# Expert layers of a four-layer gated model: results added to the tokens' rows in DRAM by indirect transfers, instead of gathered back

## The chip, the cores and the metric

The kernel runs on one core of one Trainium2 chip. The metric is device time in microseconds (us), the median of several runs. A profile of one execution goes with it; its time is a little longer than its span, which runs from the first to the last instruction recorded. Engines are named as in the profile: PE (matmuls), PEld (their weight loads), DVE (vector), ACT (scalar), POOL (GpSimd), SP (the sync engine, which here only issues transfers).

## The reference

Two sequences of 1024 tokens, 256 values each, pass through four layers. Each layer adds a gated cross-attention to 64 context rows and then a gated feed-forward part. `x` is the residual stream.

```python
x = x + jnp.tanh(g_xattn[0]) * _L0_xattn_ref(_layernorm(x), ctx_1024, ...)
x = x + jnp.tanh(g_ffn[0]) * _L0_ffn_ref(_layernorm(x), ...)     # 8 experts, each token goes to its best one
x = x + jnp.tanh(g_xattn[1]) * _L1_xattn_ref(_layernorm(x), ctx_1024, ...)
x = x + jnp.tanh(g_ffn[1]) * _L1_ffn_ref(_layernorm(x), ...)     # 8 experts, every token through all
x = x + jnp.tanh(g_xattn[2]) * _L2_xattn_ref(...)
x = x + jnp.tanh(g_ffn[2]) * _L2_ffn_ref(...)    # best expert, at most 384 tokens each
x = x + jnp.tanh(g_xattn[3]) * _L3_xattn_ref(...)
x = x + jnp.tanh(g_ffn[3]) * _L3_ffn_ref(...)    # best two experts, at most 320 tokens each
```

An expert is two matrix products with a bias and a function between them. For layer 2, with `h` the normalized tokens:

```python
logits = h @ router_w.T
probs = softmax(logits); chosen_e = argmax(probs); chosen_p = max(probs)
pos = (running count of chosen_e before this token)          # its place in the expert's buffer
kept = pos < C
out = gelu(buf[e] @ w1[e] + b1[e]) @ w2[e] + b2[e]           # buf[e]: the tokens kept for expert e
y = out[chosen_e, pos] * (chosen_p * kept)
```

Layers 0 and 3 are alike, without a limit in layer 0, and with two choices per token and normalized weights in layer 3. All of it is float32.

## The kernel before

The residual stream stays in the chip's SBUF for the whole run, as `xs`: 16 tiles of 128 tokens, in four groups of four (`NT` = 16, `NG` = 4). The layers follow each other in program order. A framework orders each engine's instructions and sets the waits; its planned times decide how instructions of neighbouring parts interleave. A transfer is issued from the queue of an engine: SP for plain ones, ACT for a few constants, POOL for indirect ones, which take one row per index. Each queue is worked off in order, so an instruction that waits holds what is behind it.

Layers 0, 2 and 3 send tokens to experts, in the same steps:

- `normed` (L185) normalizes all groups (`norm_group`, `stats`): `h` by token, `hT` transposed. `keep_tokens` (L703) writes `h` to a DRAM buffer `hd`, from SP.
- `route` (L608) computes for each token its expert, its weight and its rank among the expert's tokens. From these comes a slot number: the row of the token in the experts' buffers.
- `invert` (L671) turns "slot of each token" into "token of each slot" by matmuls with one-hot matrices (`ohl`, `ohh`; L685 to L695). The result, `idx` (L700), holds for every slot of 128-row tiles the number of its token; an unused slot gets 0.
- `gather_T` (L711) gathers the tokens of a tile from `hd` by an indirect transfer on POOL (L716), transposes them on PE (L725) and copies them to `xT` on DVE and ACT (`evac`, L138).
- `ffn` (L729) does the two products (`ps_m`, through `mm256`, L193; then `ps_y`, L741), adds the bias on DVE (`y_ff`, L746) and writes the tile from SP to a DRAM buffer `yb` (L747).
- `combine` (L750), after all experts: for each tile of tokens and each choice it gathers the results' rows from `yb` (L756, POOL) and adds them, times the weight, to `xs` (L760, DVE). `yg` has four buffers.

In layer 0 (`moe0`, L784) the tokens of an expert fill whole tiles, 23 in all (`L0_NTILE`). Which expert's weights a tile needs is known only on the chip, so the weights are gathered too, by POOL (`rows_of`, L841): two of 1 MB (`w`), and two small ones (`b1j`, `b2j`). In layers 2 and 3 (`moe_capacity`, L864) each expert has three tiles (128, 128, 128 rows; 128, 128, 64 in layer 3), and weights are loaded from SP (`load_w`). `wpool` has six weight buffers, `xgp` six token buffers, `yp` four result buffers.

After layer 0's experts stand the set-up of the next attentions (`heads1.setup`, `xattn2_setup`), `combine`, and the middle (L1135): layer 1 with its dense experts, and the attention of layer 2, worked off by groups; `group` (L541, L600) writes the last update of `xs` there. Weights of the middle are loaded from SP (L991, L994). After layer 2's experts follow the attention of layer 3 (`heads_xattn`) and its experts, whose last lines send `xs` to the output from SP (L1206).

Of the kernel before, what the change touches and what calls it, by code (L numbers as in the profile page):

```python
# [17 lines left out]
P = 128  # L18
B, S, D = 2, 1024, 256
SK = 64  # L20
N = B * S
# [20 lines left out]
def kernel(ctx: ExitStack, tc: tile.TileContext, a: dict, out: bass.AP):  # L42
# [34 lines left out]
    partid = int_ramp([P, 1], [[0, 1]], 0, 1, "partid")  # L77
    rev8 = int_ramp([P, E], [[-1, E]], E, 0, "rev8")
# [592 lines left out]
    def invert(one, pm, slots, ntile):  # L671

        ps = pm.tile([P, 512], F32, name="ps_m")
        for i, slot in enumerate(slots):
# [13 lines left out]
            ohh = one.tile([P, NT, ntile], F32, name="ohh")  # L688
            V.tensor_tensor(
                ohh, ramp[:, :ntile].unsqueeze(1).to_broadcast([P, NT, ntile]),  # L690
                bc(hi, ntile), ALU.is_equal,
            )
            V.tensor_mul(ohh, ohh, bc(tokid, ntile))
            for t in range(NT):
                T.matmul(  # L695
                    ps[:, :ntile], lhsT=ohl[:, t, :], rhs=ohh[:, t, :],
                    start=(i == 0 and t == 0), stop=(i == len(slots) - 1 and t == NT - 1),
                )
        idx = one.tile([P, ntile], I32, name="idx")
        V.tensor_copy(idx, ps[:, :ntile])  # L700
        return idx

    def keep_tokens(hs, name):  # L703
        hd = dram.tile([N, D], F32, name=name)
        for g in range(NG):
            nc.sync.dma_start(
                hd[g * GW : (g + 1) * GW, :].rearrange("(t p) d -> p t d", p=P), hs[g]
            )
        return hd

# [18 lines left out]
    def ffn(pools, xT, w1, w2, b1, b2, widths, func, yb, row0):  # L729
# [8 lines left out]
        for w in widths:  # L738
# [8 lines left out]
            nc.sync.dma_start(yb[row0 + at : row0 + at + w, :], y[:w, :])  # L747
            at += w

    def combine(yp, yb, choices):  # L750

        for t in range(NT):
            xt = xs[:, t, :]
            for slot_i, wgt in choices:
                yg = yp.tile([P, D], F32, name="yg")
                G.indirect_dma_start(  # L756
                    out=yg, out_offset=None, in_=yb[:, :],
                    in_offset=bass.IndirectOffsetOnAxis(ap=slot_i[:, t : t + 1], axis=0),
                )
                V.scalar_tensor_tensor(xt, yg, wgt[:, t : t + 1], xt, ALU.mult, ALU.add)  # L760
# [23 lines left out]
    def moe0():  # L784
        with ExitStack() as es:
# [3 lines left out]
            hd = keep_tokens(hs, "hd0")  # L789
# [29 lines left out]
            slot_i = one.tile([P, NT], I32, name="slot0_i")  # L819
            V.tensor_copy(slot_i, slot)  # L820
# [18 lines left out]
            idx = invert(one, pm, [slot], L0_NTILE)  # L839
# [8 lines left out]
            yb = dram.tile([L0_NTILE * L0_W, D], F32, name="yb0")  # L848
# [462 lines left out]
```

## Time and profile before

| | us |
|---|---|
| median of three runs | 2472.63 (2470.77 to 2479.15) |
| the profiled execution | 2466.53 |
| its span | 2464.7 |
| PE busy | 2173.3 (88%) |
| DVE busy | 1259.3 (51%) |
| POOL busy | 1019.3 (41%) |
| ACT busy | 755.6 (31%) |
| L741 PE, products `ps_y` | 252.8 |
| L756 POOL, gathers of results | 61.6 in 64 instructions |
| L760 DVE, adding them to `xs` | 38.9 in 64 instructions |
| L716 POOL, gathers of tokens `xg<-hd_L` | 45.1 in 48 instructions |

Rows of groups give the line, engine and operation, what is written and read, how many there are, the busy time, the mean of one in ns, and the engine's idle time ahead of them with what ended most of it. A POOL row of an indirect transfer is the time of its issue, not of the transfer. The chain that ended last is followed back from the last instruction; in order of time, each line has a start, a length and the engine or transfer that was waited for. In a table of windows every stretch of time has its length, then each engine's busy time and number of instructions, the granted PE clock, the busy share of the 16 DMA engines, and GB/s.

### The profile page before, as it was taken

How to read it: one execution, taken by the hardware profiler on the slowest of the kernel's cores; microseconds unless marked ns; L12 is line 12 of the kernel's file. 1: busy time of each engine (PE TensorE's matmuls, PEld its weight loads, DVE VectorE, ACT ScalarE, POOL GpSimd, SP SyncE). 2: the span in 40 equal slices, each digit the busy share in tenths (PEclk: the TensorE clock that was granted, in tenths of full speed). 3: DMA queues.
4: the chain of work that ended last, by engine and by line, in shares of the span. 5: the costliest groups of instructions: out<-in, count | busy, mean ns of one | idle time of the engine just before them, and what ended most of it. 6: DMA issues, size and time to landing. Idle time of an engine off the chain costs nothing.

```text
span 2464.7 us, 27973 instructions
## 1 busy us (share of the span) xinstructions
PE 2173.3 (88%) x10132; PEld 1776.8 (72%) x10132; DVE 1259.3 (51%) x2725; ACT 755.6 (31%) x1431; POOL 1019.3 (41%) x1220
## 2 busy tenths in 40 slices
PE   5569995999999999999999999999779968878991
PEld 3268883688888788887788878888567745566771
DVE  7940005676566866566756565656620028651002
ACT  1003430443333533335333343333212213221220
POOL 3315555146666356663466655666111020001104
PEclk9759996899999999999999999999869989867995
DMA  2028982012322122321222222222413440012313
GB/s 84 0 71 301 312 309 88 9 60 87 92 87 77 44 77 88 91 87 49 73 90 90 86 78 82 89 86 86 137 54 124 120 143 5 9 44 75 124 52 108
DMA packets 91177, 232.20 MB, mean 94 GB/s; under 512 B 13792, under 2 KB 32736, under 8 KB 80672
## 3 DMA queue, kind: packets, MB, share of 16 engines
q1 hardware_dynamic: 71216, 157.70, 20.2%
q0 software_dynamic: 14816, 68.53, 8.5%
q10 hardware_dynamic: 5008, 4.18, 0.5%
q8 instruction: 81, 1.33, 0.2%
q14 instruction: 56, 0.46, 0.1%
HBM read 213.20 MB, written 17.17 MB: 93 GB/s over the span
## 4 chain that ended last, share of the span: by engine, by line
PE 77%; DVE 9%; DMA 3%; issue 3%; POOL 3%; ACT 2%; DVEq 0%; POOLq 0%; ACTq 0%; SPq 0%
PE ps_b L1022 13%; PE ps_m L193 11%; PE ps_y L741 10%; PE ps_a L1022 9%; PE ps_e L1022 9%; PE ps_b L1067 6%; PE ps_a L1067 4%; PE ps_e L1067 4%; PE ps_y L429 2%; PE ps_y L193 2%; DMA yg<-yb_L,at_i 1%; PE ps_tr L181 1%; PE ps_y L381 1%; PE ps_m L695 1%; DVE st L149 1%
## 5 line engine op out<-in xcount | busy, mean ns | idle before, releaser
L1022 PE MATMUL ps_b<-xsum,w 128*128 128x256 f32 x1536 | 386.9, 380 | 2.3 <-DVE c L1048 2.2
L1022 PEld LDWEIGHTS ps_b<-xsum,w 128*128 128x128 f32 x1536 | 289.4, 190 | 47.1 <-issue 4.6
L929 POOL TENSOR_TENSOR w<-w 128x256 f32<-128x256 f32 x192 | 141.1, 735 | 382.2 <-DMA w<-in_L_Wu_dram 193.9
L1022 PE MATMUL ps_a<-hT,w 128*128 128x256 f32 x1024 | 268.6, 382 | 0.6 <-DVE hT L142 0.6
L193 PE MATMUL ps_m<-xT,w 128*128 128x128 f32 (+2 forms) x1248 | 247.9, 358 | 13.8 <-DVE xT L142 13.7
L741 PE MATMUL ps_y<-w,mid 128*128 128x256 f32 (+1 forms) x1136 | 252.8, 379 | 0.0
L193 PEld LDWEIGHTS ps_m<-xT,w 128*128 128x128 f32 x1248 | 183.4, 195 | 73.1 <-DVE xT L142 21.3
L741 PEld LDWEIGHTS ps_y<-w,mid 128*128 128x128 f32 (+1 forms) x1136 | 206.6, 184 | 38.9 <-issue 2.7
L974 ACT COPY u<-ps_b 128x512 f32<-128x512 f32 (+1 forms) x192 | 98.7, 514 | 406.9 <-PE ps_b L1067 260.7
L1022 PEld LDWEIGHTS ps_a<-hT,w 128*128 128x128 f32 x1024 | 193.3, 191 | 29.7 <-issue 3.2
L746 DVE TENSOR_TENSOR y_ff<-ps_y,b 128x256 f32<-128x256 f32 (+1 forms) x48 | 20.3, 423 | 312.7 <-PE ps_y L741 312.7
L716 POOL DMA_INDIRECT xg<-hd_L,idx x48 | 45.1, 939 | 319.8 <-PE ps_tr L725 180.7
L930 POOL TENSOR_TENSOR w<-w 128x256 f32<-128x256 f32 x192 | 167.7, 873 | 0.1
L931 POOL TENSOR_TENSOR w<-w 128x256 f32<-128x256 f32 x192 | 165.3, 861 | 0.0
L932 POOL TENSOR_TENSOR w<-w 128x256 f32<-128x256 f32 x192 | 158.9, 828 | 14.4
L1022 PE MATMUL ps_e<-xsum,w 128*128 128x256 f32 x512 | 133.6, 382 | 0.0
L1022 PE MATMUL ps_e<-hT,w 128*128 128x256 f32 x512 | 133.2, 380 | 0.0
L1067 PE MATMUL ps_b<-t,w 128*128 128x256 f32 x512 | 131.8, 381 | 0.9 <-DVE accT L1085 0.9
L1067 PE MATMUL ps_a<-b,w 128*128 128x256 f32 x512 | 132.0, 379 | 0.0
L956 ACT COPY ps_b<-ps_a 128x512 f32<-128x512 f32 (+1 forms) x192 | 96.1, 501 | 108.5 <-DVE b L1052 64.1
L1084 POOL TENSOR_TENSOR m<-m,accT 128x256 f32<-128x256 f32 x60 | 72.1, 1201 | 126.5 <-ACT m L962 112.8
L1049 DVE TENSOR_TENSOR b<-b,c 128x512 f32<-128x512 f32 x128 | 116.1, 907 | 3.8
(300 smaller groups left out, 3785.0 us busy)
## 6 DMA issues: line engine op xcount, KB each, us to landing
w<-in_L_Wg_dram SPq DMA_DIRECT2D x64, 512.0 KB
w<-in_L_Wu_dram SPq DMA_DIRECT2D x64, 512.0 KB
w<-in_L_Wd_dram SPq DMA_DIRECT2D x64, 512.0 KB
w<-in_L_W_dram SPq DMA_DIRECT2D x32, 1024.0 KB
yb_L<-y_ff SPq DMA_DIRECT2D x40, 128.0 KB
hd_L<-h SPq DMA_DIRECT2D x8, 512.0 KB
yb<-y_ff SPq DMA_DIRECT2D x23, 128.0 KB
xs<-in_x_dram SPq DMA_DIRECT2D x4, 512.0 KB
```

The source lines that it names most:

```text
L193: T.matmul(ps, lhsT=lhs(c), rhs=rhs(c), start=(c == 0), stop=(c == n - 1))
L741: T.matmul(ps[:w, :], lhsT=mid[:, f, at : at + w], rhs=w2[:, f, :], start=(f == 0), stop=(f == NF - 1),)
L929: G.tensor_add(s[0], a21, a22)
L930: G.tensor_sub(s[1], s[0], a11)
L931: G.tensor_sub(s[2], a11, a21)
L932: G.tensor_sub(s[3], a12, s[1])
L956: A.copy(self.b, self.pa)
L974: A.copy(u2, self.b)
L1022: T.matmul(ps[:, q * 256 : (q + 1) * 256], lhsT=lhs[kind][:, q, :], rhs=xr[kind], start=(first and q == 0), stop=True, skip_group_check=True,)
L1049: V.tensor_mul(m[name], m[name], c)
L1067: T.matmul(ps, lhsT=wd[kind][:, q, :], rhs=m["rhs"][kind][:, q * 256 : (q + 1) * 256], start=(clear and q == 0), stop=True, skip_group_che ...
L1084: G.tensor_add(sb, sb, acc[:, i, j])
```

## The change

Each expert layer first writes the residual stream to a second DRAM buffer `xd` (`keep_rows`, which takes the place of `keep_tokens`). `invert` also returns the weight of each slot (`wsl`), by twice as many columns in its matmuls. `ffn` multiplies a result tile by these weights on DVE and adds its rows to their tokens' rows of `xd`, with one indirect, adding transfer on POOL. Unused slots have weight zero; `idx` sends slot row p of them to a spare row N + p, so that the rows of one transfer are distinct, and both buffers have 128 such rows, zeroed. `combine` and `yb` are gone. At the end of layers 0 and 2 `xs` is reloaded from `xd`; at the end of layer 3 `xd` is copied to the output, from SP and ACT.

```diff
+    spare = int_ramp([P, 1], [[0, 1]], N, 1, "spare")
+    tokoff = int_ramp([P, NT], [[P, NT]], -N, 1, "tokoff")
+    zeros = const.tile([P, D], F32, name="zeros")
+    V.memset(zeros, 0.0)
...
-    def invert(one, pm, slots, ntile):
+    def invert(one, pm, slots, wgts, ntile):
...
-            ohh = one.tile([P, NT, ntile], F32, name="ohh")
+            ohh = one.tile([P, NT, 2, ntile], F32, name="ohh")
...
-            V.tensor_mul(ohh, ohh, bc(tokid, ntile))
+            V.tensor_sub(lo, tokoff, lo)
+            V.tensor_mul(ohh[:, :, 0], ohh[:, :, 1], bc(lo, ntile))
+            V.tensor_mul(ohh[:, :, 1], ohh[:, :, 1], bc(wgt, ntile))
             for t in range(NT):
                 T.matmul(
-                    ps[:, :ntile], lhsT=ohl[:, t, :], rhs=ohh[:, t, :],
+                    ps[:, : 2 * ntile], lhsT=ohl[:, t, :],
+                    rhs=ohh[:, t].rearrange("p a j -> p (a j)"),
...
-        V.tensor_copy(idx, ps[:, :ntile])
-        return idx
-
-    def keep_tokens(hs, name):
-        hd = dram.tile([N, D], F32, name=name)
+        V.tensor_scalar(idx, ps[:, :ntile], spare, None, ALU.add)
+        wsl = one.tile([P, ntile], F32, name="wsl")
+        V.tensor_copy(wsl, ps[:, ntile : 2 * ntile])
+        return idx, wsl
+
+    def keep_rows(name, parts):
+
+        hd = dram.tile([N + P, D], F32, name=name)
         for g in range(NG):
             nc.sync.dma_start(
-                hd[g * GW : (g + 1) * GW, :].rearrange("(t p) d -> p t d", p=P), hs[g]
-            )
+                hd[g * GW : (g + 1) * GW, :].rearrange("(t p) d -> p t d", p=P), parts(g)
+            )
+        nc.sync.dma_start(hd[N:, :], zeros)
         return hd
+
+    def residual(g):
+        return xs[:, g * TG : (g + 1) * TG, :]
+
+    def reload(xd):
+        for g in range(NG):
+            nc.sync.dma_start(
+                residual(g), xd[g * GW : (g + 1) * GW, :].rearrange("(t p) d -> p t d", p=P)
+            )
...
             V.tensor_add(y[:w, :], ps[:w, :], b2[:w, :])
-            nc.sync.dma_start(yb[row0 + at : row0 + at + w, :], y[:w, :])
+            V.tensor_scalar_mul(y[:w, :], y[:w, :], wsl[:w, j0 + s : j0 + s + 1])
+            G.indirect_dma_start(
+                out=xd[:, :],
+                out_offset=bass.IndirectOffsetOnAxis(ap=idx[:w, j0 + s : j0 + s + 1], axis=0),
+                in_=y[:w, :], in_offset=None, compute_op=ALU.add,
+            )
             at += w
-
-    def combine(yp, yb, choices):
...
-            hd = keep_tokens(hs, "hd0")
+            hd = keep_rows("hd0", lambda g: hs[g])
+            xd = keep_rows("xd0", residual)
...
-            combine(yp, yb, [(slot_i, wgt)])
+            reload(xd)
...
             if then:
                 then(pm, "ps_m")
-            combine(yp, yb, choices)
+                reload(xd)
+        return xd
...
-    moe_capacity("L3", 2, e_bias[:, 1, :], 2, L3_CAP, 7, AF.Relu)
-
-    ov = out.rearrange("b (t p) d -> p (b t) d", p=P)
+    xd = moe_capacity("L3", 2, e_bias[:, 1, :], 2, L3_CAP, 7, AF.Relu)
+
+    of = out.rearrange("b s d -> (b s) d")
     for g in range(NG):
-        nc.sync.dma_start(ov[:, g * TG : (g + 1) * TG, :], xs[:, g * TG : (g + 1) * TG, :])
+        eng = nc.sync if g % 2 else nc.scalar
+        eng.dma_start(of[g * GW : (g + 1) * GW, :], xd[g * GW : (g + 1) * GW, :])
```

## The prediction

> **What bounds the kernel now.** I read the page's shares first (PE busy 88% of the span), then the chain of waits in order of time, to find the places where PE is not what ends last. Three lie around this change: the ends of the three expert layers, where results are gathered back. The table of windows gives each expert loop and what follows it up to PE's next real work (for layer 3, up to the end).
>
> ```profile
> core 0: us, PE busy (x) PEld busy (x) DVE busy (x) ACT busy (x) POOL busy (x), PEclk, DMA share, GB/s
> 184.40:374.90 190.50, 175.74 (x1153) 159.27 (x1154) 14.09 (x46) 73.42 (x207) 104.89 (x111) 0.98 0.86 298
> 375.30:420.00 44.70, 14.35 (x68) 10.18 (x67) 30.60 (x65) 0.06 (x1) 33.62 (x40) 0.60 0.37 121
> 1828.40:2009.00 180.60, 175.73 (x694) 128.16 (x695) 15.01 (x33) 42.13 (x73) 20.74 (x22) 0.98 0.39 121
> 2009.00:2039.30 30.30, 4.39 (x21) 2.88 (x20) 19.61 (x72) 0.34 (x1) 15.25 (x16) 0.61 0.44 143
> 2242.10:2413.00 170.90, 165.34 (x686) 119.67 (x686) 14.06 (x32) 37.13 (x72) 19.61 (x21) 0.98 0.28 91
> 2413.00:2464.70 51.70, 0.00 (x0) 0.00 (x0) 15.50 (x32) 0.00 (x0) 30.49 (x32) 0.52 0.46 123
> ```
>
> The loops (rows 1, 3, 5) are PE's, with little else near its limit in layers 2 and 3. Layer 0's loop is different: DMA share 0.86. The exits (rows 2, 4, 6) last 44.7, 30.3 and 51.7 us with PE nearly or wholly idle. The chain inside the last exit says what fills it:
>
> ```profile
> 2413.00 1.90 DMA yb_L<-y_ff
> ...
> 2415.76 2.21 DMA yg<-yb_L,at_i
> ...
> 2423.27 2.99 DMA yg<-yb_L,at_i
> ...
> 2429.52 4.95 DMA yg<-yb_L,at_i
> ...
> 2456.09 2.90 DMA yg<-yb_L,at_i
> ```
>
> One landing of the last result, then 32 gathers at POOL's pace: a gather lands 2.2 to 3.0 us after its start, 5 us when others are in flight. Last, POOL's queue in layer 0's loop, which the change lengthens:
>
> ```profile
> 230.56 0.95 POOL L842 DMA_INDIRECT b2j<-in_L_b_dram,ex_i  x1 [2.07 <-DVE xT L142]
> 231.81 0.95 POOL L716 DMA_INDIRECT xg<-hd,idx  x1 [0.30 <-issue]
> 233.06 0.94 POOL L842 DMA_INDIRECT w<-in_L_W_dram,wrow  x1 [0.30 <-issue]
> 234.31 0.94 POOL L842 DMA_INDIRECT w<-in_L_W_dram,wrow  x1 [0.30 <-PE ps_m L193]
> 235.55 0.95 POOL L842 DMA_INDIRECT b1j<-in_L_b_dram,wrow  x1 [0.30 <-issue]
> 238.57 0.94 POOL L842 DMA_INDIRECT b2j<-in_L_b_dram,ex_i  x1 [2.06 <-DVE xT L142]
> ```
>
> Five issues of 0.95 + 0.30 = 1.25 us make 6.25 us of an 8.01 us tile; POOL idles 2 us, then waits for the tile's end.
>
> **What the Trainium skill says.** "DMA: Bandwidth & Descriptors", section "SDMA does more than copy": an add during a transfer is done by a compute unit in the data stream; no rate is given, and no run here shows one yet. Section "Rules for kernel authors": nothing holds the destination between an accumulate's read and write, so the earlier DMA's semaphore must be waited for. The built order has that: each scatter on POOL waits for the one before to land. Section "Queues, rings and completion order": an engine takes a ring's descriptors in order. The trace agrees: the last gather of layer 0 stood behind weight loads on POOL's queue and landed after 5.30 us.
>
> **The change, part by part.** The profiled execution took 2466.53 us for a span of 2464.7; the median of the runs is 2472.63, so 6.1 above. I sum against the former.
>
> (1) Layer 3's exit. Removed: 51.7 us. Added: the weight multiply, 0.4 (128x256, as h L173 at 0.35, plus its wait); the last scatter; the copy to the output. Scatter: unknown. Below, a gather's 2.2 us; above, I carry 12. I take 3.5, a gather's 2.2 to 3.0 plus a destination read. The three last scatters start 3.5 us apart (PE's 3.46 us per tile), so they just don't queue. The output now goes DRAM to DRAM, 4 x 512 KB on two queues. Not in the trace; the page's section "Latency and other measured facts" gives about 210 GB/s per direction for copies between HBM tensors: 2.1 MB is 10 us (estimate), plus 2.0 fixed (its section on the SWDGE path). Below: 6 us, engines at 8 KB in 0.31 us; above: 20. Sum 0.4 + 3.5 + 12 + 0.1 = 16. Gain 51.7 - 16 = 35.7.
>
> (2) Layer 0's exit. After: multiply, behind one setup instruction on DVE, 0.8; scatter 3.5; reload of the first 512 KB, 4.0 (the last out DMA, issued at 2460.74, ended the span at 2464.7); norm of four tiles on DVE, 4 x (0.40 + 0.16) + about 2 of small ones + 4 x 0.35 = 6; setup instructions mixed into it (kT, vT, wos), 2.5; transposes and hT 2.3. Sum 19.1 against 44.7: gain 25.6. Setup's matmuls lie inside this; the first DVE statistic stands before the last setup instructions, so they too wait for the reload, which is why I add their 2.5. The reload stands before the next weights on SP: they issue some 5 us later, are needed some 40 us on, and hide behind attention.
>
> (3) Layer 2's exit. Multiply and setup 0.8, scatter 4.5 (a 1 MB weight load runs beside it), reload 4, norm 6 with 2 of the next group's mixed in, transposes and hT 1.8: 19 against 30.3. About 1 to 2 us of norm work that was done between gathers now comes later, on a busy DVE. Gain 10.
>
> (4) Layer 0's loop. POOL gets a sixth issue: 7.5 of 8.0 us, still under. But the built order puts xg of tile j+2 behind scatter j, and scatter j behind y_ff j and the landing of scatter j-1. Behind it queue b1, b2, xg and the next weights. From tile j's last matmul: scatter at +1.05, b1 2.3, b2 3.55, xg 4.8; the transposes that read it start at +7.84 at today's pace. So a gather has 3.0 us, where it had 5.9 before; in the last seven tiles w2 and a multiply ahead of xT come between too, and it has 1.8. And 2 MB of weights ahead in the ring take 7 us at 298 GB/s. I get 0.2 to 0.5 us late per tile, which the longer tile then partly forgives, 0.8 in the last seven: loss 8 us (bounds 0, and 35 at 1.5 us per tile). Unlike before, yb's 128 KB writes on SP are gone, which pays for part of the scatter's traffic.
>
> (5) Before each loop, invert. Per slot one more multiply of ohh (0.55) and a small subtract (0.17), less a cast: 0.6 on the way to idx, four slots: +2.5. The matmuls grow from 24 to 48 columns; they are 0.22 us apart, as are those with 256 columns, so the width is free; if not, 4 x 1 us.
>
> (6) Costed at nothing: the copy of xs to xd. In layer 0 its four issues precede hd on SP at about 130 us, 50 us before the first gather. In the middle they would block weight loads on SP if xs were late: counted through the built order, they stand after loads issued at 874.5, 1197.3 and 1474.1, xs is ready at 875.7, 1206.2 and 1481.1, and the next loads issue at 881.0, 1207.6 and 1483.9. Free, by a margin of 1 to 5 us; without it, a stall of a few us at PE. Zero rows: six writes while SP only waits. The multiply in layers 2 and 3 stands after xT in DVE's order, DVE busy 8%. Scatters in layers 2 and 3: one each 7.0 to 7.3 us, against 3.5; gathers are two experts ahead.
>
> Sum: 35.7 + 25.6 + 10 - 8 - 2.5 = 61. 2466.5 - 61 = 2405.7 against the profile, 2411.8 against the median. I say 2408.
>
> **The rivals.** (A) Layer 0's loop turns from PE-bound to bound by POOL's order and ring: a tile of 9.5 us, gain (2) lost. For: 0.86 DMA share and 0.5 us of POOL left; an accumulating issue may cost POOL more than 0.95. Against: weights are two tiles ahead, and a longer tile loosens the ring. Cost 35 instead of 8: 2435.
> (B) Tails longer: scatter 6 us, output 20. The last three scatters then queue (+7.5), the other exits lose 2.5 each, the output 8: 2428.
> (C) Slower: the serialized scatters set the pace. 24, 24 and 23 of them follow each other by landing; a landing of x us costs 24(x - 7.3) + 24(x - 7.0) + 23(x - 8.0) once above these. It eats the 61 us at about 8.1 us; at 10, 2600. For it: reading and writing rows in DRAM for each of 128 rows, whose rate nothing shows. Against: a 128 KB write with 1 KB packets passes the engines in 0.5 us here, so it would have to be over ten times that.
> (D) No change: all exits are refilled by later waits; PE then starts no earlier. Layer 3's exit speaks against it: nothing follows it.
>
> **How the numbers follow.** Forecast 0.62 (its own range 2388 to 2425); A 0.17, B 0.10, C 0.08, D 0.02, 0.01 for mixtures below the range. 2385 to 2445 leaves out C, D and half of the worse A: just under 2 in 10. Faster 0.90, same 0.02, slower 0.08, with 0.3% (7.4 us) as what a measurement can tell.
>
> **What would show it.** Last y_ff to span's end about 16 us, not 51.7; PE's next start after layers 0 and 2 about 19 us on, not 44.7 and 30.3; layer 0's tile period 8.0 to 8.5 us, its lost time before ps_tr, waiting for xg; scatter landing about 3.5 us. Wrong if a scatter lands after over 7 us, if POOL's scatter issue is well over 1 us, or if ps_tr waits over 1 us per tile.

## The result and the profile after

The changed kernel takes 2448.96 us (median of four runs, 2438.26 to 2454.52); the kernel before, run on the same chip, takes 2471.8. The ratio is 0.9896, 95% interval 0.9857 to 0.9935. A second set of six runs gave 2454.42 against 2471.46, ratio 0.9936 (0.9913 to 0.9959). So it is faster, by 17 to 23 us (0.6 to 1.0 per cent) and not by the 64 forecast, and the time lies above the range given (2385 to 2445).

The table of windows of the kernel after, cut as in the prediction: each expert loop, and what follows it up to PE's next real work (for layer 3, up to the end). Only the loops of layers 2 and 3 are cut otherwise: they start here at the first token gather, some 3 us ahead of where the prediction's rows start, so rows 3 and 5 are not to be set against those; the large table below has one cut for all.

```profile
core 0: us, PE busy (x) PEld busy (x) DVE busy (x) ACT busy (x) POOL busy (x), PEclk, DMA share, GB/s
188.90:406.93 218.03, 184.45 (x1156) 162.66 (x1157) 22.49 (x68) 74.06 (x207) 140.89 (x132) 0.96 0.82 258
406.93:431.80 24.87, 14.73 (x70) 9.66 (x68) 18.27 (x51) 0.58 (x1) 10.80 (x15) 0.68 0.65 217
1849.50:2033.33 183.83, 176.39 (x694) 128.51 (x695) 22.61 (x56) 42.28 (x73) 58.85 (x47) 0.97 0.45 119
2033.33:2055.90 22.57, 4.27 (x21) 3.09 (x20) 13.64 (x65) 0.12 (x1) 2.78 (x2) 0.66 0.64 198
2261.50:2437.12 175.62, 166.88 (x688) 120.44 (x688) 21.48 (x55) 37.28 (x72) 58.80 (x47) 0.97 0.35 89
2437.12:2452.70 15.58, 0.00 (x0) 0.00 (x0) 0.35 (x2) 0.00 (x0) 1.43 (x1) 0.59 0.49 147
```

The exits (rows 2, 4, 6) shrank from 44.7, 30.3 and 51.7 us to 24.9, 22.6 and 15.6: 63.6 us won. Layer 0's loop (row 1) grew from about 191 to 218 us: 27 lost, with POOL's busy time up from 105 to 141 us. The table below cuts the whole span the same way for the kernels of this study, from each one's profiled execution (us; loops run from the issue of the first token gather to the last `y_ff`; the columns of one row sum to the span).

| kernel | to 1st gather | loop 0 | exit 0 | layer 1 and entry of 2 | loop 2 | exit 2 | attention 3 and entry | loop 3 | exit 3 | span |
|---|---|---|---|---|---|---|---|---|---|---|
| before | 184.4 | 190.9 | 44.7 | 1405.9 | 183.1 | 30.3 | 199.1 | 174.6 | 51.7 | 2464.7 |
| before_again | 180.7 | 191.9 | 44.7 | 1413.1 | 184.5 | 30.3 | 198.4 | 175.7 | 52.1 | 2471.4 |
| after | 188.9 | 218.0 | 24.9 | 1417.7 | 183.8 | 22.6 | 205.6 | 175.6 | 15.6 | 2452.7 |
| after_again | 187.9 | 216.0 | 26.3 | 1417.6 | 184.1 | 22.9 | 205.6 | 175.6 | 15.5 | 2451.5 |
| l0_gathers_back | 191.5 | 198.7 | 44.4 | 1415.4 | 183.4 | 22.6 | 193.0 | 174.9 | 17.7 | 2441.6 |
| layers2and3 | 185.0 | 191.5 | 44.2 | 1412.8 | 183.4 | 22.4 | 196.7 | 174.9 | 17.5 | 2428.4 |
| layer3_alone_2 | 182.2 | 190.2 | 43.9 | 1411.9 | 184.9 | 30.0 | 193.5 | 175.0 | 15.9 | 2427.5 |
| scatter_behind_one_bias | 191.2 | 187.5 | 22.0 | 1415.3 | 184.4 | 22.6 | 205.9 | 175.7 | 15.4 | 2420.0 |

Against the forecast's own base (2466.53 to 2405.7, 61 us) the first profile after, 2454.52, won 12.0. The 48.8 missing are: loop 0, 19.1 (27.1 lost, 8 forecast); layer 1 and attention 3, 18.3 (11.8 and 6.5, none forecast); exit 0, 5.8; exit 2, 2.3; loops 2 and 3, 1.7; the stretch to the first gather, 2.0 (4.5, if the 2.5 forecast for the inversions of all three layers are set against it); less 0.4 that exit 3 did better.

This is the timeline of POOL's queue in the middle of layer 0's loop in the kernel after (start, duration, engine, line, operation; in brackets the idle time before and what ended it):

```profile
302.79 1.62 POOL L772 DMA_INDIRECT xd<-y_ff,idx  x1 [1.89 <-DVE y_ff L771]
304.71 0.99 POOL L858 DMA_INDIRECT b1j<-in_L_b_dram,wrow  x1 [0.30 <-issue]
306.01 0.95 POOL L858 DMA_INDIRECT b2j<-in_L_b_dram,ex_i  x1 [0.30 <-issue]
307.27 0.95 POOL L739 DMA_INDIRECT xg<-hd,idx  x1 [0.30 <-issue]
308.52 0.95 POOL L858 DMA_INDIRECT w<-in_L_W_dram,wrow  x1 [0.30 <-PE ps_y L765]
311.52 1.62 POOL L772 DMA_INDIRECT xd<-y_ff,idx  x1 [2.05 <-DVE y_ff L771]
```

The adding transfer occupies POOL for 1.62 us, where the gathers take 0.95. It also waits for its own tile's `y_ff`, and while it waits for 1.9 us nothing behind it is issued. The idle time that POOL had before `b2j` stands now before the scatter (the adding transfer), and is still there. The waits of that loop (engine, tile and line, what it waited for, us in total, times, longest) show which engine waits:

```profile
PEld ps_tr L748 <- DMA xg<-hd,idx: 28.9, 19, 2.8
POOL xd L772 <- DVE y_ff L771: 27.1, 18, 3.8
```

In the kernel before, the same wait of PE's weight load for `xg` was 1.2 us in all. The tile, from `y_ff` to `y_ff`, was 8.05 us before in the mean, and is 9.28 after: 8.0 or 8.1 four times, then 8.2 to 11.4; 22 times the difference is the 27 us.

### The profile page after: what moved, and what is told of

Read it like the earlier page. It is cut to its first block, busy times and chain, and to the rows that moved or that the text cites. A ratio compares the mean times of both kernels' runs of the same rounds, so it can differ in the third digit from the quotient of the medians.

```text
span 2452.7 us, 27852 instructions
## 1 busy us (share of the span) xinstructions
PE 2199.9 (90%) x10132; PEld 1787.2 (73%) x10132; DVE 1255.2 (51%) x2742; ACT 757.9 (31%) x1431; POOL 1072.5 (44%) x1229
## 4 chain that ended last, share of the span: by engine, by line
PE 74%; DVE 11%; DMA 5%; POOL 3%; issue 2%; ACT 2%; POOLq 0%; ACTq 0%; DVEq 0%; SPq 0%
PE ps_b L1036 12%; PE ps_m L198 10%; PE ps_e L1036 8%; PE ps_a L1036 8%; PE ps_y L765 8%; PE ps_b L1081 6%; PE ps_a L1081 4%; PE ps_e L1081 4%; PE ps_y L198 3%; PE ps_y L434 2%; DMA xg<-hd,idx 2%; PE ps_m L704 1%; PE ps_tr L186 1%; DMA xd_L<-y_ff,idx 1%; PE ps_y L386 1%
## 5 line engine op out<-in xcount | busy, mean ns | idle before, releaser
L943 POOL TENSOR_TENSOR w<-w 128x256 f32<-128x256 f32 x192 | 140.8, 734 | 404.0 <-DMA w<-in_L_Wu_dram 174.6
L198 PE MATMUL ps_m<-xT,w 128*128 128x128 f32 (+2 forms) x1248 | 253.8, 364 | 11.8 <-DVE xT L147 11.7
L198 PEld LDWEIGHTS ps_m<-xT,w 128*128 128x128 f32 x1248 | 188.5, 200 | 71.9 <-DVE xT L147 19.3
L772 POOL DMA_INDIRECT xd_L<-y_ff,idx x48 | 74.9, 1561 | 232.4 <-DVE y_ff L771 135.8
L145 ACT COPY xT<-ps_tr 128x128 f32<-128x128 f32 (+2 forms) x39 | 13.4, 344 | 355.7 <-PE ps_tr L748 289.4
```

Source lines behind the costliest of these rows:

```text
L198: T.matmul(ps, lhsT=lhs(c), rhs=rhs(c), start=(c == 0), stop=(c == n - 1))
L772: G.indirect_dma_start(out=xd[:, :], out_offset=bass.IndirectOffsetOnAxis(ap=idx[:w, j0 + s : j0 + s + 1], axis=0), in_=y[:w, :], in_offse ...
L943: G.tensor_add(s[0], a21, a22)
```

## The experiments

The first question was whether all the loss lies in layer 0's loop, and then what makes it: the time of the adding transfer itself, the place of the token gather behind it, or POOL's time.

### The kernels again, and layer 0 with its gathers back

`after_again` and `before_again` have no edit. `l0_gathers_back` leaves the change in layers 2 and 3, and in layer 0 writes result rows with plain transfers and gathers them at the end, as before:

```diff
+            if idx is None:
+                nc.sync.dma_start(xd[j0 + at : j0 + at + w, :], y[:w, :])
...
-            reload(xd)
+            combine(yp, yb, [(slot_i, wgt)])
```

> The changed kernel a second time, unaltered. It ran 9 us longer in the middle (layer 1 and layer 2's attention, 1369 against 1360 us) than the kernel before, with PE's granted clock 0.98 against 0.99 there. Theory: that part is the clock of that one execution; the middle then takes another length here (1358 to 1366 us if the clock is 0.99), while layer 0's loop stays at 215 to 220 us, its exit near 25, layer 3's exit near 15.5. Rival: the copies of the residual stream to DRAM among the middle's weight loads cost the 9 us; the middle is again 1367 to 1371 us at any clock.

> The kernel before once more, for a second profile. Theory: the middle (1406 us with the entry to layer 2's experts, against 1413 to 1418 in five profiles with the change) and layer 3's attention (199 against 193 to 206) are a matter of where PE's half-clock periods fall; here they differ by 4 us or more from the first profile of the same kernel in at least one of the two, and by as much as the sum of the clock not granted differs. Rival: the change itself makes the middle longer; then it is 1404 to 1408 us here again.

> Layer 0 alone goes back to writing its tiles to a buffer and gathering them; layers 2 and 3 keep the adding transfers. Theory: the missing gain was lost in layer 0's loop, to POOL's queue. The loop is 191 us again (218 in the changed kernel), the exit 44 to 45 us (25), the first gather 1 to 2 us earlier: 2440, some 9 us better than the changed kernel. Rival: layer 0 gained more by its exit than its loop lost, and the rest went into the middle or the clock: the loop stays over 210 us, and the time is 2465 to 2470.

Measured: `after_again` as told above; `before_again` 2473.67 against 2473.43 (ratio 1.0002, 0.9988 to 1.0015); `l0_gathers_back` 2442.2, ratio 0.9888 (0.9858 to 0.9918). Loop 0 goes back from 216 to 198.7 us and exit 0 from 26 to 44.4: in layer 0 the change gives at the exit about what it takes in the loop. The two profiles of the kernel before also differ: layer 1 took 1405.9 us in one and 1413.1 in the other. Of the 18 us that seemed lost in layer 1 and attention, 7 are the first profile's good luck; more on this below.

### Does adding cost more than writing?

`l0_plain_rows` writes the rows in layer 0 at the same indices without adding, so the residual is left out of that layer's result.

```diff
-                in_=y[:w, :], in_offset=None, compute_op=ALU.add,
+                in_=y[:w, :], in_offset=None, **({"compute_op": ALU.add} if add else {}),
```

> Layer 0's scatters write their rows instead of adding them: the residual stream of layer 0 is left out of the sum, everything else is as in the changed kernel, the order of the instructions too. Theory: the issue on POOL is shorter without the add (1.0 us for 1.6), and the gather behind it is issued 0.6 us earlier; the loop gains about 0.6 us in each of 20 tiles, 205 us, 2437. Rival 1: the add itself, a read and a write at each row, makes the transfers slow; landings fall from a median of 5.1 us to 3 or less, and the loop to 191 to 196 us, 2425. Rival 2: the issue costs 1.6 us because it is an indirect write, add or not; the loop stays at 215 to 220 us, 2449.

Measured: 2441.67, ratio 0.9876 (0.9843 to 0.9908); loop 0 211.3 us. The view of the tile `xd` in it:

```profile
L772 POOL DMA_INDIRECT xd<-y_ff,idx x23: 985/992/1007, 206.9 to 403.6; - x23
DMA to landing us min/median/max: 2.4/5.5/7.0
```

and in the kernel after:

```profile
L772 POOL DMA_INDIRECT xd<-y_ff,idx x23: 1582/1620/1635, 204.4 to 407.9; - x23
DMA to landing us min/median/max: 3.8/5.6/7.8
```

Adding costs POOL 0.63 us more per issue, but in the median lands as soon as a plain write. Taking it away gives back 7 of the 27 us. The add in DRAM is not what makes most of the loss: some 20 us are left with plain writes too.

### Fetches moved ahead of the scatter

`token_gathers_ahead` issues each token gather three tiles ahead; `biases_ahead_too` also both bias gathers.

```diff
+                while len(ahead) < min(j + 1 + AHEAD, L0_NTILE):
+                    ahead.append(gather(xgp, hd, idx, len(ahead), [L0_W]))
...
-                gather_T(xgp, xT, pt, hd, idx, j, [L0_W])
+                gather_T(xgp, xT, pt, hd, idx, j, [L0_W], ahead[j])
```

> Layer 0's token gathers are written three tiles ahead of the tile that uses them, so that the gather behind scatter j in POOL's order is that of a tile about five later. The same instructions, all scatters kept. Theory (place in POOL's order: the gather stands behind a scatter that waits for its tile): the waits of the transposes for their tokens nearly vanish, the loop is 192 to 198 us instead of 218, bounded by 8.15 us of POOL issue per tile; 2426. Rival 1 (adding transfers slow the other transfers down): the loop stays at 215 us or more, 2449. Rival 2 (POOL has too much to issue, order does not matter): the tile stays at 9 us or more with POOL never idle, 2440 or more.

> As the kernel with layer 0's token gathers three tiles ahead, where the wait only moved to b1j (ACT waited 89 us for it: it was issued behind the scatter and landed behind 2 MB of weights). Here b1j and b2j are gathered three tiles ahead too, in six buffers; the same instructions, another order. Theory (what hurts is what stands in POOL's queue behind a scatter with too little lead): no engine waits for b1j or xg any more, and the loop falls from 214 us to what POOL can issue, 8.15 us a tile and 13 us ahead of the first result: 192 to 200 us; the whole 2422 to 2430. Rival 1 (adding transfers slow the others down): the wait goes on to the weights, and the loop stays at 207 us or more. Rival 2 (POOL is the bound at more than its issue times, because it still waits for each tile's result): period 8.8 us or more, loop 205 us or more, POOL's idle time ahead of the scatters 1 us a tile or more.

Measured: 2439.03, ratio 0.9876 (0.984 to 0.9912), loop 0 213.8 us; and 2475.63, ratio 1.001 (0.9995 to 1.0024), loop 0 242.8. The wait only changed its name. In the waits of `token_gathers_ahead` in that loop the first layer's activation waits for its bias:

```profile
ACT mid L766 <- DMA b1j<-in_L_b_dram,wrow: 89.1, 17, 8.2
```

and in those of `biases_ahead_too` PE waits for weights:

```profile
PEld ps_m L199 <- DMA w<-in_L_W_dram,wrow: 37.5, 10, 5.5
POOL xd L778 <- DVE y_ff L777: 66.3, 15, 6.5
```

In these orders some fetch that is needed two tiles on still stands behind the scatter, and that one is late. The prediction's wait for `xg` was one name of this, not the cause.

### One issue fewer, and the scatter moved behind the fetches

`one_bias_gather` keeps the fetches ahead and gets both biases with one gather from a joined table, so that a tile has five issues again, the scatter among them. `one_bias_gather_only` joins the tables in the changed kernel and moves nothing by hand.

```diff
-                b1 = rows_of(two.tile([P, NF], F32, name="b1j"), "L0_b1", wrow, j)
-                b2 = rows_of(two.tile([P, D], F32, name="b2j"), "L0_b2", ex_i, j)
+                b12 = rows_of(two.tile([P, NF + D], F32, name="b12j"), "L0_b12", wrow, j)
+                b1, b2 = b12[:, :NF], b12[:, NF:]
```

`scatter_behind_fetches` leaves six issues and orders each scatter behind all fetches for the tile three on; `scatter_behind_one_bias` does both.

```diff
+                if j + 3 < L0_NTILE:
+                    held_j.append(fetch(j + 3))
+                with ExitStack() as after:
+                    for q in queued:
+                        after.enter_context(tc.issue_after(q.ins))
+                    add_rows(xd, idx, ys)
```

> As before, with both biases of an expert laid out in one row, so that one gather fetches both: POOL issues five transfers a tile again (6.9 us), not six (8.15). Theory: POOL has slack, PE is the bound, the loop 188 to 193 us as in the kernel before; the whole 2417 to 2424. If POOL's sum was no part of the cause, the loop is the same as that of the kernel with the biases ahead, within 2 us. If adding transfers slow down the weights, it stays above 205.

> The changed kernel with both biases in one gather and nothing else: scatter j still stands ahead of the bias and token gathers of tile j+2, DVE's order is as in the changed kernel, POOL issues 6.9 us a tile. Rival (the sum decides): with 1.1 us of slack in 8.0 the loop is 190 to 196 us, the whole 2420 to 2428. Theory (the waiting scatter decides): the gather still comes late, only 1.25 us less so; periods of 8.4 to 8.8 us, loop 199 to 208 us, the whole 2430 to 2438.

> The six transfers of a tile as in the changed kernel, but in this order on POOL: first the weight, b1j, b2j, token gather and second weight of tile j+3 (the last waits for tile j's last product), then scatter j, forced behind them. A scatter is thus ready when its turn comes, and nothing waits behind one that waits. Theory (a scatter that waits for its tile at the head of POOL's queue delays whatever fetch stands behind it): tiles follow each other every 8.15 to 8.3 us, POOL's issue times, from first to last, start-up 13.5 us; the loop 193 to 197 us against 218; the whole 2422 to 2430. Rival 1 (adding transfers slow the fetches in the DMA engines): periods stay at 9 us or more. Rival 2 (six issues are too many in any order): POOL's issues alone take over 8.5 us a tile, loop 202 us or more.

> The same order, with both biases in one gather: five issues, 6.9 us of POOL a tile. Theory: PE sets the pace again, 8.0 us a tile, the loop 190 to 192 us as before the change, with the scatters in it; the whole 2415 to 2422, the best so far. If the order mattered little and the number of issues alone, it is as the kernel with one bias gather in its earlier order, 202 us and 2430.

| run | median | ratio (interval) | loop 0 | mean tile |
|---|---|---|---|---|
| one_bias_gather | 2429.83 | 0.9842 (0.981 to 0.9873) | 202.1 | 8.43 |
| one_bias_gather_only | 2428.21 | 0.9804 (0.9754 to 0.9855) | 202.0 | 8.56 |
| scatter_behind_fetches | 2445.2 | 0.9888 (0.9849 to 0.9927) | 210.6 | 8.86 |
| scatter_behind_one_bias | 2421.41 | 0.98 (0.9769 to 0.9831) | 187.5 | 7.91 |

With both together the loop is as short as before. The timeline of POOL's queue in `scatter_behind_one_bias`:

```profile
302.80 1.62 POOL L787 DMA_INDIRECT xd<-y_ff,idx  x1 [1.12 <-issue]
304.72 0.98 POOL L872 DMA_INDIRECT w<-in_L_W_dram,wrow  x1 [0.30 <-issue]
306.01 0.95 POOL L872 DMA_INDIRECT b12j<-in_L_b_dram,wrow  x1 [0.30 <-issue]
307.27 0.95 POOL L740 DMA_INDIRECT xg<-hd,idx  x1 [0.30 <-issue]
308.52 0.95 POOL L872 DMA_INDIRECT w<-in_L_W_dram,wrow  x1 [0.30 <-PE ps_m L198]
310.20 1.62 POOL L787 DMA_INDIRECT xd<-y_ff,idx  x1 [0.73 <-issue]
```

and its loop in the table of windows:

```profile
191.20:378.73 187.53, 176.43 (x1156) 160.24 (x1157) 22.21 (x68) 68.11 (x207) 119.85 (x110) 0.98 0.91 297
```

The scatter is issued 7.4 us after the last one, nobody waits behind it for a `y_ff` that is not there, and PE's busy time is back at 176 us, at DMA share 0.91. All 23 adding transfers are in this loop, each waiting for the one before to land; so neither their landing nor their traffic stretches the tile by itself. This is the fastest kernel of the study with `one_bias_gather_only`, whose interval overlaps with it.

That one says more than its mean. 15 of its 22 tiles take 8.0 us although the scatter still waits for its `y_ff` ahead of the fetches, so a waiting scatter in front doesn't by itself stretch a tile. The planner also moved something: behind scatter j stands the token gather of tile j+3, where the changed kernel has that of tile j+2, so the run doesn't separate the fifth issue from the longer lead. Its three long tiles (11.7, 13.3 and 12.3 us) are the three in which PE's built order has a transpose of the next tile ahead of this tile's products; it waits there 2.4, 4.3 and 3.4 us for `xg`. The second of them, in the timeline of PE:

```profile
310.06 0.38 PE L748 MATMUL ps_tr<-ident,xg 128*128 128x128 f32 x2
314.74 0.45 PE L748 MATMUL ps_tr<-ident,xg 128*128 128x128 f32 x1 [4.30 <-DMA xg<-hd,idx]
```

The joined table was not tried on the kernel before, so how much of its gain belongs to the change alone is open.

### Is it the order on DVE?

In the built order the multiply by the weight stands behind the copies to `xT` in part of the loop. `multiply_first` orders it ahead of the next tile's gather and transposes; `multiply_first_pinned` also holds the fetches where the changed kernel has them.

```diff
+                with ExitStack() as behind:
+                    if j:
+                        behind.enter_context(tc.issue_after(scaled[-1].ins))
+                    gather_T(xgp, xT, pt, hd, idx, j, [L0_W])
```

> The same move on DVE, POOL's order left to the planner, which now puts the token gather of tile j+2 right ahead of scatter j (both weights, b1j, gather, scatter j, b2j). No gather stands behind the scatter of its own round. Theory: what is left is POOL's issue, 8.15 to 8.3 us a tile; loop 193 to 198 us, the whole 2425 to 2430. Rival: six issues leave no slack, every late landing is kept to the end, and the period is 8.6 us or more, loop 204 us or more.

> The changed kernel with one thing moved: on DVE the multiply of tile j's result is issued ahead of the copy of xT of tile j+1 (in the changed kernel it stands behind it in tiles 1 to 14). POOL's order is pinned to that of the changed kernel's first tiles: both weights, scatter j, b1j, b2j, token gather of tile j+2. Theory (a closed ring: the gather of tile j+1 lands, xT, then the multiply, scatter j, two small fetches, the gather of tile j+2; 8.7 us by the parts, 10.1 with a weight between): with the multiply ahead of xT the ring is gone; what is left goes over two tiles, from y_ff j through scatter, fetches, gather, products to y_ff j+2, 16.9 us or 8.45 a tile. Loop 196 to 202 us, the scatters issued 1 us after y_ff; the whole about 2432. Rival (POOL's queue by itself, wherever DVE puts the multiply): periods as in the changed kernel, 8.9 to 9.6 us from the sixth tile on, loop 212 us or more.

Measured: 2450.96, ratio 0.9888 (0.9853 to 0.9924), and 2455.12, ratio 0.9923 (0.9896 to 0.9949); loop 0 218.8 and 220.6 us. No gain: DVE's order is not the cause. In these loops the transposes' waits for `xg` are all but gone (behind the first tile PE waited for it not at all and for 2.5 us, and for 21.3 in the changed kernel), and the loops are as long: the lateness of `xg` alone doesn't set them either.

### A sixth issue in the kernel before

Two edits of the kernel before, with no scatter in them. `sixth_idle_gather` adds a bias gather to each tile that nobody reads; `result_write_on_pool` moves the result's write from SP's queue to POOL's.

```diff
+                rows_of(two.tile([P, NF], F32, name="b1x"), "L0_b1", wrow, j)
```

```diff
-            nc.sync.dma_start(yb[row0 + at : row0 + at + w, :], y[:w, :])
+            (eng or nc.sync).dma_start(yb[row0 + at : row0 + at + w, :], y[:w, :])
```

> The kernel before with a sixth issue on POOL per tile of layer 0 that nothing waits for and that waits for nothing late: a second gather of the small b1 rows into a buffer that is not read. POOL then issues 7.5 us a tile. If only the sum of POOL's issues counts and its limit is PE's 8.0 us, the loop stays at 190 to 193 us. If POOL loses more than its issue times, so that six are too many, it is 200 us or more.

> The kernel before with the write of each result tile of layer 0 issued from POOL instead of SP: a plain transfer, no indices, no adding, no multiply, but a sixth issue that waits for y_ff, with the second weight, b1j, b2j and the next token gather behind it. About 7.5 us of issue a tile. Theory (a waiting issue in POOL's order costs, whatever it transfers): periods over 8.6 us, loop 204 us or more. Rival (the sum of issues against 8.0 us decides, 8.15 in the changed kernel being over it): 7.5 us fit, loop 190 to 195 us.

Measured, one run each beside 2472.41: 2499.4, loop 0 223.0 us, a tile of 9.48; and 2490.85, loop 0 210.8 us, a tile of 8.99. A gather that nobody waits for costs more than the whole change did in this loop. Part of that is PE's clock: the window tables give 0.94 for its loop and 0.98 for the kernel before, an estimated 9 to 10 of the 32 us. POOL's queue in `sixth_idle_gather`:

```profile
299.97 0.95 POOL L842 DMA_INDIRECT b2j<-in_L_b_dram,ex_i  x1 [2.12 <-DVE xT L142]
301.22 0.94 POOL L842 DMA_INDIRECT b1x<-in_L_b_dram,wrow  x1 [0.30 <-issue]
...
306.29 0.94 POOL L842 DMA_INDIRECT b1j<-in_L_b_dram,wrow  x1 [0.39 <-ACT mid L736]
309.37 0.94 POOL L842 DMA_INDIRECT b2j<-in_L_b_dram,ex_i  x1 [2.13 <-DVE xT L142]
```

Six issues take 7.5 us, and POOL still idles 2.1 us before `b2j`, as it did with five: the idle time moved along with the tile. Set side by side, POOL's issues per tile (each with its 0.30 us gap) and the tile:

| run | issues per tile, us | tile, us |
|---|---|---|
| before | 6.25 | 8.05 |
| result_write_on_pool | 6.25 + 0.88 = 7.13 | 8.99 |
| sixth_idle_gather | 6 x 1.25 = 7.5 | 9.48 |
| l0_plain_rows | 6.25 + 1.30 = 7.55 | 8.97 |
| after | 6.25 + 1.92 = 8.17 | 9.28 |
| scatter_behind_fetches | 8.17 | 8.86 |
| one_bias_gather | 5.0 + 1.92 = 6.92 | 8.43 |
| scatter_behind_one_bias | 6.92 | 7.91 |

A tile is 1.1 to 2.0 us longer than its issues in the rows where an issue waits for the tile's last results with fetches behind it in the queue, and 0.7 to 1.0 us longer in the two where the scatter stands behind all fetches. (`token_gathers_ahead`, with 9.09 us for 8.17, would be 0.9 in the first group, so the two are not far apart.) The number of issues divides the runs more sharply: every kernel with six of them in a tile has a mean tile of 8.86 us or more, whatever the sixth does and wherever it stands, and every kernel with five one of 8.71 or less. That the 2 us were no slack for a sixth issue is shown. Why they were not is not wholly shown: that the buffers make a ring (a `b2j` buffer comes free with `y_ff`, and the fetches behind it feed the next `y_ff`) is my reading of the releasers. In `sixth_idle_gather`, PE's matmuls waited 31.5 us for `xT` (10.9 in the kernel before), and `y_ff` and both copies to `xT` start together 1.2 us after the transposes' modelled end; no view names what holds them. That stays open.

### One part of the change alone

`layer3_alone` has the change only in layer 3, but with the new constants and helpers built as in the changed kernel. `layer3_alone_2` has layers 0 and 2 in the old form throughout, and `layers2and3` layer 0.

```diff
+            if idx is None:
+                nc.sync.dma_start(yb[row0 + at : row0 + at + w, :], y[:w, :])
+            else:
+                V.tensor_scalar_mul(y[:w, :], y[:w, :], wsl[:w, row0 + s : row0 + s + 1])
```

> Adding transfers in layer 3 alone; layers 0 and 2 write tiles and gather them back as before the change. Theory: layer 3's exit falls from 52 to 15.5 us and nothing else changes but some 1 us in layer 0's inversion and 1 us in layer 3's loop; 2473 - 36 + 2 = 2439, within the 6 us that the clock moves. Rival: what layer 3 saves at its end is lost again in its attention and loop, where the residual stream is copied and POOL issues scatters; 2455 or more.

> Adding transfers in layer 3 alone again, now written into the kernel before, so that POOL's order in layers 0 and 2 is that of the kernel before, transfer by transfer. In the first try the planner had put the fetches of layer 0 in another order, and that loop stalled twice (two tiles of 15 us, loop 205 us for 191). Theory: loop 191 us, layer 3's exit 15.5 us for 52, all else as before within the clock's 5 us; 2473 - 36 + 1 = 2438. Rival: the gain of the exit is lost again in layer 3's own attention and loop; 2455 or more.

> Adding transfers in layers 2 and 3, layer 0 as before the change with its order kept. Theory: the loop of layer 0 is 191 us and its exit 44.7; layer 2's exit 22.7 for 30.3, layer 3's 15.5 for 52; 2473 - 36.4 - 7.5 + 2 = 2431, some 20 us better than the whole change: in layer 0 it costs more (27 in the loop, 1 in the inversion) than its exit gives (19). Rival: layer 0's part is worth its 19 us and the whole change is held back by the clock or the middle alone; then this is no better than the whole change, 2450 or more.

Measured: 2462.89, ratio 0.9958 (0.9942 to 0.9974); 2438.4, ratio 0.9844 (0.9828 to 0.986); 2435.02, ratio 0.9835 (0.9814 to 0.9857). The first misleads: with its constants built early, the planned order in layer 0, which should not have changed, did, and loop 0 took 205.3 us. POOL has `b1j` ahead of `xg` there and the weights' issues split, and with that most tiles still take 8.0 us; the loss lies in two tiles of 15.6 and 15.2, in which PE's order again has a transpose one tile early and waits 5.3 and 5.4 us for `xg`. `l0_gathers_back` (198.7) has the same two, of 11.0 and 14.9 us. In the clean kernels loop 0 is the old one, here in `layers2and3`:

```profile
185.00:376.50 191.50, 176.41 (x1156) 159.96 (x1157) 14.45 (x46) 73.63 (x207) 104.99 (x111) 0.98 0.85 296
```

So layer 3 alone gives 39.7 us of the 2478.11 that the kernel before took beside it, layer 2 some 3 more, and `layers2and3` is faster than the whole change: by 15 to 25 us, when each is taken by its ratio (0.9835 against 0.9896 and 0.9936). Not all of that is layer 0. Of the 24.3 us between the two profiles 11 lie in layer 0, up to the end of its exit (26.5 in the loop and 3.9 ahead of it, less 19.3 in the exit), and 14 in layer 1 and attention 3, which have the same code in both; the clock, below, differs there.

## Why the prediction was wrong, step by step

**Sign and layer 3's exit: right.** Step (1), layer 3's exit at 16 us, measured 15.6. The chain of the kernel after near its end (start, duration, what), and then the last scatter and the first issues of the copy to the output in the timelines of POOL and SP:

```profile
2430.75 3.69 DMA xd_L<-y_ff,idx
...
2435.20 3.79 DMA xd_L<-y_ff,idx
```

```profile
2439.72 1.43 POOL L772 DMA_INDIRECT xd_L<-y_ff,idx  x1 [2.96 <-DMA xd_L<-y_ff,idx]
2442.96 1.22 SPq L1221 DMA_DIRECT2D out_dram<-xd_L  x2
```

The scatters land in 3.7 to 3.8 us (forecast 3.5) and do queue behind one another, where the prediction had them just not queue: they start 4.5 us apart, and the last one 2.2 us after its tile was ready. The copy to the output takes 9.7 us from its issue to the end, where 12 was taken: 2.1 MB in 9.7 us are 216 GB/s, which agrees with the rate of about 210 that the prediction used, and leaves no room for the 2.0 us of fixed cost that it added from a section on transfers issued from POOL (the copy is issued from SP and ACT). So the parts are right in kind, but the sum is so close because two misses of about 2 us cancel.

**Step (4), layer 0's loop: this step failed.** "POOL gets a sixth issue: 7.5 of 8.0 us, still under" was wrong twice, and the loop lost 27.1 us where 8 were forecast. The scatter's issue was taken at a gather's 0.95 and measured 1.62, so that the sum is 8.17 and over the tile; and the sum was the wrong test, since one idle gather at 0.95, with which it is 7.5, already makes the tile 9.48. The prediction itself quoted POOL waiting 2.07 us for the tile's end before `b2j`, and read it as time to spare. The loss lies inside the bounds of 0 to 35, but the value taken in them, 8, came from counting the lead of one gather instead of asking whether POOL can take a sixth issue at all. (Some 5 of the 27 us are PE's clock, an estimate from 0.96 and 0.98 in the window tables.) Rival A, POOL's order setting the tile at 9.5 us, is what the tile became (9.28), with its "against" refuted: a longer tile loosened nothing. It was given 0.17. Two of the prediction's own signs of being wrong came true: a scatter's issue well over 1 us, and waits of `ps_tr` over 1 us in a tile (28.9 us in 19).

One reading behind the prediction doesn't hold. The last gather of layer 0, which landed after 5.30 us, did not stand mainly behind weights on POOL's queue: from 361.4 to 367 us the transfers of SP's queue took 63% of the DMA engines' time and those of POOL's queue 20%.

**Step (2), layer 0's exit: mechanism right, size off.** 24.9 us, forecast 19.1. The scatter landed in 3.75 and the reload in 4.71, 1.0 above the terms' sum; the larger part of the 5.8 is the norm. These are small operations on DVE while POOL sums weight tiles, from the timelines of the two engines in the kernel after:

```profile
422.19 0.17 DVE L161 TENSOR_SCALAR yi<-yi 128x4 int32<-128x4 int32 x1
422.35 0.72 POOL L943 TENSOR_TENSOR w<-w 128x256 f32<-128x256 f32 x1 [12.89 <-DMA w<-in_L_Wg_dram]
422.39 0.69 DVE L165 TENSOR_TENSOR q<-yi 128x4 f32<-128x4 f32 x1
424.49 0.16 DVE L165 TENSOR_TENSOR q<-rstd 128x4 f32<-128x4 f32 x1
425.97 0.65 DVE L165 TENSOR_TENSOR q<-rstd 128x4 f32<-128x4 f32 x1
```

The same operation on a 128x4 tile takes 0.16 or 0.65 us, and the long ones begin with POOL's. The Trainium skill, "SBUF — State Buffer", section "Who interferes with whom", says that a DVE operation with two SBUF inputs and a GpSimd operation that reads SBUF use one port in turn, the second blocked for a whole instruction; 0.65 beside POOL's 0.72 agrees. No run tested it.

**Step (3), layer 2's exit:** 22.6 us, forecast 19. The chain of the kernel after there:

```profile
2027.09 5.13 DMA xd_L<-y_ff,idx
...
2032.97 5.56 DMA xd_L<-y_ff,idx
...
2039.27 3.71 DMA xd_L<-y_ff,idx
2042.99 4.07 DMA xs<-xd_L
```

The last `y_ff` was there at 2033.33, its multiply done at 2034, but its scatter started at 2039.27: beside 1 MB weight loads from SP the two before it took 5.1 and 5.6 us, and scatters go one by one. The term "scatter 4.5" was 9; the norm and transposes behind it took 8.8 us, 1 less than forecast. Rival B's queue was therefore real here, though with a landing under 6 us.

**Step (5), inversion:** the columns were free (32 matmuls in 7.06 us, 7.02 before) and the added work in layer 0 about 0.9 us on DVE, where 0.6 was forecast for each slot. The 4.5 us that the stretch to the first gather grew come from elsewhere: layer 0's own attention, whose code the change leaves alone, ends 6.7 us later (its last norm is transposed from 135.29 on, 128.59 before), and a better clock gives part of it back. `layers2and3`, which builds its new constants later, has 129.24; that the constants move the planned order is likely, but no run tests it. **Step (6), copies:** free, as said: layer 1, in which they stand, is as long as before once its clock is taken off. That clock had no step at all.

**The clock of PE.** Layer 1 is untouched by the change, and took 1405.9 us before and 1417.7 after. Windows of 2 us in the same stretch of it; after:

```profile
884.00:886.00 2.00, 0.69 (x4) 0.29 (x2) 2.00 (x4) 0.36 (x1) 1.92 (x2) 1.00 0.00 0
886.00:888.00 2.00, 1.99 (x6) 1.47 (x7) 2.00 (x5) 0.00 (x0) 0.21 (x1) 0.74 0.00 0
888.00:890.00 2.00, 2.00 (x5) 1.17 (x5) 0.29 (x1) 0.00 (x0) 0.00 (x0) 0.50 0.00 0
...
896.00:898.00 2.00, 2.00 (x8) 1.66 (x7) 0.42 (x1) 1.65 (x2) 1.16 (x2) 0.70 0.00 0
```

and before:

```profile
870.00:872.00 2.00, 0.68 (x3) 0.28 (x3) 2.00 (x4) 0.36 (x1) 1.92 (x2) 1.00 0.00 0
872.00:874.00 2.00, 2.00 (x8) 1.28 (x8) 2.00 (x5) 0.00 (x0) 0.14 (x1) 1.00 0.00 0
```

The same gap, with PE busy for 0.69 and 0.68 of 2 us, is followed by half clock until about 897 in one execution and by none in the other. Over the whole of layer 1, (1 - granted clock) x its length, summed over windows of 5 us, is 39.1 us before, 46.1 in `before_again`, 50.1 after and 37.9 in `one_bias_gather`; taken off the stretch's length, it leaves 1366.8, 1367.0, 1367.6 and 1369.1. So nearly all of the 11.8 us are clock and not work, and the kernel before's first profile happened to lose little. Attention 3 takes 193.0 to 205.9 us over these kernels, with clock sums of 28.5 to 48.1; what is left, 157 to 165, is less even there and goes the other way, so its 6.5 us are put down to the clock with less certainty. The Trainium skill, "TensorE: Matmul & The Clock Gate", section "🔬 Part 1: The HAM clock gate (the "warmup" mystery)", gives a clock that is half or whole and an activity window that runs freely, not from the start of the work; half clock for some 10 us after one gap of 1.3 us and none after the other fits a window whose phase matters, and that a shift upstream moves this phase is inferred, not shown. In loop 0 it adds to the loss: PE has a gap at each wait for `xg`, the granted clock is 0.96 there (0.98 before), and PE's busy time rose from 175.7 to 184.5 us.

## What to carry to other kernels

Before giving a queue one more issue, don't only add its durations up against the period: look for an issue in it that waits for the period's own last result. The queue's idle time just before such a wait may be part of the loop and not to spare, and a fetch behind it that is needed soon may be late; one idle issue, tried first, would have told. Here one issue fewer, by a joined bias gather, turned a ratio of 0.990 into 0.980, with the scatter moved behind the fetches or without; without it three tiles were long for another reason. An exit that was many small gathers is well replaced by adding transfers where the queue has room, as in layers 2 and 3, and a kernel with only part of a change must be looked at for orders that moved elsewhere, on POOL and on PE.

## What the runs showed of the hardware that was not expected

- An indirect adding transfer of 128 rows of 1 KB takes 1.43 to 1.63 us of POOL to issue, a plain indirect write 0.99, a gather 0.95, a plain direct write 0.58. In flight adding costs nothing to be seen: medians 5.6 and 5.5 us beside weight gathers at DMA share 0.8, and 3.7 with little else under way.
- A gather of a tile's bias that nobody reads, once in a tile, made the program 27 us longer, and its loop 32 (one run; some 10 of these are clock, by the estimate above).
- Equal gaps of PE, of 1.32 us each, are followed by some 10 us of half clock or by none, and this moved a stretch of 1400 us by 7 us between two executions of one kernel (1405.9 and 1413.1).
- In some tiles the last activations of `mid` come 1.43 us apart (0.37 busy, 1.06 waiting for PE) instead of 0.45, in the kernel before too. What causes it stays open.
